# Gated delta-rule attention in one megakernel: outputs and gates with channels on the partitions, square sums in column tiles, roots spread by DMA

## The chip, the core and the metric

The kernel runs on one core of a Trainium2 chip, as one program. Its metric is the device time of one execution, in microseconds (us). The core has five engines that run side by side: TensorE (PE in the profile, with PEld for its weight loads), VectorE (DVE), ScalarE (ACT), GpSimd (POOL), and SyncE (SP), which here only issues DMA transfers. Each engine takes its instructions in the order in which they were written. Everything is float32.

## The reference, cut to what matters

The input x has 4 sequences of 256 tokens with 256 channels; the attention sees it as 2 sequences of 512. The first layer's attention is a chunked gated delta rule with 16 key heads and 32 value heads of 128 channels. Its end is what the change concerns:

```python
core = chunk_gated_delta_rule(q, k, v, g, beta)
out = core * rsqrt(mean(core * core, -1, keepdims=True) + EPS) * norm_w
out = out * silu(z)                 # z = x @ w_z, one gate per output channel
return out.reshape(Bb, Ss, VAL_DIM) @ w_out
```

Around it stand "conditioning" steps (a two-way scan over time that gives a ratio by which a sigmoid of x is multiplied), a mixture of 64 small experts, a gated mixing layer and a mixture of 8 experts. The results are added to x.

## The kernel before

**Tiling.** The 1024 tokens are two halves s = 0, 1 of 512 tokens (two sequences b of 256, each two chunks n of 128). A `Unit` is one key head with its two value heads v in one half: 32 units. Four units are a `Group`, and two consecutive units are a pair that shares the inverse of the triangular matrix and the output projection. Tiles are 128 partitions by 512 elements.

**One unit.** `products` loads `wqk`, makes q and k with channels on the partitions (`convolved`: matmul `ps_cvq`, `ps_cvk`, then a scaled copy on ACT and three taps on DVE), applies silu, makes the products of q and k (`ps_gram`), and takes the square sums of q and k by matmuls of 32 columns of ones (`ps_kt`, four column tiles), turned by a DVE transpose of 32x32 blocks. It also builds the decay matrices `attnT` from a broadcast read of `G`. `values` makes v in the same way, transposes it on PE (`ps_vt`) so that tokens stand on the partitions, and scales it by `kn` into `vo`. `outputs` runs the delta rule: `ps_vn`, copied to `vn`; `ps_at` for chunk 0, copied over `vo[0]`; `vd` (POOL); `ps_ks`; `ps_vn` for chunk 1; `ps_at` for chunk 1 (two products per problem), copied over `vo[1]`. Tokens are on the partitions in all of these. The gates `zs` come from `gates`: matmul `ps_z` with tokens on the partitions, then silu on ACT. For a few units of the first half (`EARLY`) they are made early, stored and read back.

`normed` takes square sums on ACT (eight activations with accumulation into `rs`, through `junko`), adds `eo` and takes the power -1/2 on POOL, multiplies `vo` by the roots and then by `zs` on POOL, and transposes on PE (`ps_ot`); ACT copies the result to `oT`, scaled by `normw`, with channels on the partitions. `Group.project` multiplies `oT` by `wo` for both units of a pair (`ps_wo`, eight matmuls of 512 columns) and DVE adds the result to x.

**The order.** Nothing is issued as it is written in the code. Every step is an `op` of a `Tape` with its engine, its cost, the buffers that it reads and writes, sometimes a due time and an activation table. `Tape.plan` places all steps by their urgency, with weights in a line of constants (`SWITCH`, `SPARE`, `IDLE`, `THIN` and others), 59 shared buffers of 128x512 (`PLACES`, with a limit for each use in `MOST`) and six PSUM buffers; `pushed` works out new urgencies from the plan, and `run` repeats this `ROUNDS` times and takes one of the plans. Then all steps are issued in the order of their planned starts, and the engines keep that order. The planned times are only used for the order. Since every step is recorded through one helper, all rows of the profile show its line, and steps are told apart by their tiles.

The rest of the program (`Rest`: experts, mixing) is planned on the same tape; that of the first half fills the time beside the attention of the second half, and that of the second half ends the program.

Of the kernel before, what the change touches and what calls it, by code (L numbers as in the profile page):

```python
# [12 lines left out]
ALU = mybir.AluOpType  # L13
# [168 lines left out]
class Tape:  # L182
# [222 lines left out]
    def run(self):  # L405
        latest, plans = self.urgency(), []
        for n in range(ROUNDS):
            last = self.plan(latest)
            if last is None:
                break  # L410
            plans.append((last, n, [(o.start, o.end, o.new) for o in self.ops]))
            latest = self.pushed(last)
        for o, (o.start, o.end, o.new) in zip(self.ops, min(plans)[2]):
            pass
        for o in sorted(self.ops, key=lambda o: (o.start, o.order)):
            for buf in o.new:
                buf()
            o.emit()


ROUNDS, SWITCH, LOAD, SPARE, AHEAD, EACH, END, IDLE, MOMENT, GAP, RATE, GIVES = 10, 14.532, 1.3, 95.787, 163.973, 23.222, 1300.0, 54.829, 0.668, 62.664, 3.14, 4.877
UNIT = 42

EARLY, FEW = range(3, 5), 6
NORMS = 0.55
FOUR32, TWO64 = 0.75, 1.1
LAND = 3.0
WINDOW, ENOUGH, LITTLE, SLOW, THIN = 3.4, 0.471, 0.38, 0.5, 6.598


def _mm(n, count=1):
# [4 lines left out]
def _act(n):  # L436
    return 0.2 + 0.00078 * n


def _dve(n):  # L440
    return 0.16 + 0.00104 * n
# [354 lines left out]
class Unit:  # L796
# [85 lines left out]
    def products(self):  # L882
# [104 lines left out]
            v.reciprocal(ki().rearrange("p n b -> p (n b)"), k2())  # L987
            v.tensor_scalar(self.eo(), sums(1), 1e-6, 1e-6 * P * P, ALU.add, ALU.mult)

        op("DVE", 0.78, shifted, [ps], [turned, k2, ki, self.eo])  # L990
        op(
            "POOL",
            1.03,
# [95 lines left out]
    def values(self):  # L1089
# [17 lines left out]
        for n in range(2):  # L1107
            vo = self.buf([P, 2, 2, P], "vo", 4, name=n)
            self.vo.append(vo)
            ps = p.ps(f"vt{n}_{self.tag}")  # L1110

            def turn(n=n, ps=ps):
                for v in range(2):
                    for b in range(2):
                        at = (2 * v + b) * P
                        e.tensor.transpose(
                            ps()[:, at : at + P], accs[v]()[:, b, n * P : n * P + P], p.const(IDENT)
                        )

            op("PE", 0.44, turn, accs, [ps], to=vo)  # L1120

            def scaled(n=n, ps=ps, vo=vo):
                norms = self.kn()[:, 2 * n : 2 * n + 2].unsqueeze(1).unsqueeze(3)
                e.vector.tensor_tensor(
                    vo(),
                    ps().rearrange("p (v b d) -> p v b d", v=2, b=2),
                    norms.to_broadcast([P, 2, 2, P]),
                    ALU.mult,
                )

            op("DVE", _dve(512), scaled, [ps, self.kn], [vo])

    def outputs(self):
        p, s = self.p, self.s
# [37 lines left out]
        def decayed():  # L1172
# [1 line left out]

        op("POOL", 1.06, decayed, [vn0, self.dc], [vd])
        ps = product(
            "at0",
            lambda q: self.attnT[0]()[:, q, :],
            lambda q: vn0()[:, q, :],
            [self.attnT[0], vn0],  # L1180
        )
        copied(lambda: vob(0), ps, vo[0])
        ps = product(
            "ks",
            lambda q: cross()[:, 0, q % 2, :],
            lambda q: vd()[:, q, :],
# [36 lines left out]
        op("POOL", 1.28, queries, [cross], [qe])  # L1223
        self.zs = self.gates()
        vn1 = new_values(1, lambda: vob(1), vo[1])
        ps = p.ps(f"at1_{self.tag}")

        def second():
            for q in range(4):
                o = ps()[:, q * P : q * P + P]  # L1230
                e.tensor.matmul(o, qe()[:, q, :], vd()[:, q, :], start=True, stop=False)
                e.tensor.matmul(o, self.attnT[1]()[:, q, :], vn1()[:, q, :], start=False, stop=True)

        op("PE", 2 * cost, second, [qe, vd, self.attnT[1], vn1], [ps])
        copied(lambda: vob(1), ps, vo[1])

    def gates(self, early=False):

# [1 line left out]
        e, op = p.e, p.tape.op  # L1240
        of = []
        if self.kept:
            for n, (kept, keptb) in enumerate(self.kept):
                zs = self.buf([P, 2, 2, P], "zs", 3, name=n)
                op(
                    "SP",
                    0.45,
# [5 lines left out]
                of.append(zs)  # L1253
            return of
        wz = self.load("wz", early=early)
        for n in range(2):
            zs = self.buf([P, 2, 2, P], "zse" if early else "zs", 3, name=n)
            of.append(zs)
            ps = p.ps(f"z{n}_{self.tag}")

            def products(n=n, ps=ps):
                for b in range(2):
                    for k in range(2):
                        e.tensor.matmul(
                            ps()[:, b * 256 : b * 256 + 256],
                            p.tokens(4 * s + 2 * b + n)[:, k, :],
                            wz()[:, k, :],
                            start=k == 0,
                            stop=k == 1,
                        )  # L1270

            op("PE", _mm(256, 4), products, [wz, p.actb[s]], [ps], to=zs, few=early)

            def silu(zs=zs, ps=ps):
                e.scalar.activation(
                    zs().rearrange("p v b d -> p b v d"),
                    ps().rearrange("p (b v d) -> p b v d", b=2, v=2),
                    AF.Silu,
                )

            op("ACT", _act(512), silu, [ps], [zs], table="silu")
        return of

    def early(self):

        p = self.p
        for n, zs in enumerate(self.gates(True)):
            name = f"zs{n}_{self.tag}"
            kept = p.dram.tile([P, 2, 2, P], F32, name=name, tag=name)
            keptb = p.stays(name)  # L1290
            p.tape.op(
                "SP",
# [8 lines left out]
    def normed(self):  # L1301


        p = self.p
        e, op = p.e, p.tape.op
        vo, zs = self.vo, self.zs
        tt = e.gpsimd.tensor_tensor
        junk = self.buf([P, P], "junko", 1)
        rs = self.buf([P, 2, 2, 2], "rs", 3)

        def o(n):
            return vo[n]().rearrange("p v b d -> p (v b) d")

        def roots(n):
            return rs()[:, n].rearrange("p v b -> p (v b)")

        for n in range(2):

            def squares(n=n):
                for q in range(4):  # L1320
                    e.scalar.activation(
                        junk(), o(n)[:, q, :], AF.Square, accum_out=roots(n)[:, q : q + 1]
                    )

            op("ACT", 1.71, squares, [vo[n]], [junk, (rs, {n})])

        def shifted():
            eps = self.eo().rearrange("p (n b) -> p n b", n=2)
            tt(rs(), rs(), _over(eps, 2, 2), ALU.add)

        def root():
            flat = rs().rearrange("p n v b -> p (n v b)")
            tt(flat, flat, p.neghalf, ALU.pow)

        op("POOL", 0.22, shifted, [self.eo], [rs])
        op("POOL", 1.64, root, [], [rs])
        for n in range(2):
            op(
                "POOL",
                1.06,  # L1340
                lambda n=n: tt(o(n), o(n), _over(roots(n), 2, P), ALU.mult),
                [rs],
                [vo[n]],
            )
            op(
                "POOL",
                1.28,
                lambda n=n: tt(
                    o(n), o(n), zs[n]().rearrange("p v b d -> p (v b) d"), ALU.mult
                ),  # L1350
                [zs[n]],
                [vo[n]],
            )
        self.oT = []
        for v in range(2):
            oT = self.buf([P, 512], "oT", 4, name=v)
            self.oT.append(oT)
            ps = p.ps(f"ot{v}_{self.tag}")

            def turn(v=v, ps=ps):  # L1360
                for b in range(2):
                    for n in range(2):
                        at = (2 * b + n) * P
                        e.tensor.transpose(
                            ps()[:, at : at + P], vo[n]()[:, v, b, :], p.const(IDENT)
                        )

            op("PE", 0.44, turn, vo, [ps], to=oT)
            op(
                "ACT",  # L1370
                0.69,
                lambda oT=oT, ps=ps: e.scalar.activation(oT(), ps(), AF.Copy, scale=p.normw),
                [ps, p.normwb],
                [oT],
            )
        self.wo = self.load("wo", 2)


class Program:
# [79 lines left out]

    PLACES = 59  # L1460

    MOST = {'attnT': 20, 'kq1': 12, 'kq0': 2, 'kqm': 17, 'cross': 10, 'vo': 18, 'zs': 5, 'oT': 6, 'w0': 5, 'hw0': 9, 'w1': 8, 'hw1': 7, 'wo': 2, 'sq': 4, 'r0': 10, 'wqk': 20, 'vn': 21, 'acck': 22, 'wb0': 3, 'vd': 7, 'U': 5, 'wv': 7, 'qe': 6}

    def place(self, use, name, shape=(P, 512)):

# [55 lines left out]
    def ratio_piece(self, c, cc, b):  # L1521
# [51 lines left out]
        def both_ways(src, extra, n):  # L1573
            fw, bw = new(f"fw{n}"), new(f"bw{n}", f"bw{n}" if summed else "bw")
            op(
                "DVE",
                0.95,
                lambda: v.tensor_tensor_scan(fw(), decay, src(), 0.0, ALU.mult, ALU.add),
                [src, self.decayb],
                [fw],  # L1580
            )
            op(
                "DVE",
                0.95,
                lambda: v.tensor_tensor_scan(
                    bw()[:, ::-1], decay, src()[:, ::-1], 0.0, ALU.mult, ALU.add
                ),
# [669 lines left out]
```

## Time and profile before

| | us |
|---|---|
| median of 3 runs (lowest to highest) | 1409.51 (1408.84 to 1413.2) |
| the profiled execution's own time | 1412.93 |
| its span, first to last instruction | 1411.1 |
| TensorE's mean granted clock | 0.982 of full speed |

A row of the profile's groups gives an engine, an operation, the tile that is written and those that are read (buffer numbers left out), the shape, the count, the busy time with the mean of one in ns, and the idle time of that engine just before them. A row of DMA issues gives the count, the size of each, and the median time from issue to landing. The chain is followed back from the last instruction to what released it.

### The profile page before, as it was taken

What the parts mean: (1) busy time and instruction counts of PE and PEld (TensorE: products, weight loads), DVE (VectorE), ACT (ScalarE), POOL (GpSimd) and SP (SyncE); (2) the same over time, 40 slices, a digit from 0 to 9 for tenths busy, and PEclk for the clock granted to TensorE, in tenths of its full rate; (3) what the DMA queues carried; (4) which work ended last, traced back from release to release, by engine and by line L of the source; (5) the groups of instructions that cost most, each with busy time, mean ns of one, the idle gap of its engine ahead of it and who ended that gap; (6) DMA issues with size and microseconds to landing.
All of it is one profiled execution on the core that took longest, in us unless ns stands there. A gap on an engine that the chain in (4) does not pass through costs nothing.

```text
span 1411.1 us, 24205 instructions
## 1 busy us (share of the span) xinstructions
PE 1321.2 (94%) x8428; PEld 817.4 (58%) x8428; DVE 1064.8 (75%) x2112; ACT 915.2 (65%) x1999; POOL 922.8 (65%) x913
## 2 busy tenths in 40 slices
PE   5986999999999899999999999999999999998988
PEld 3544766765875676766676576555455544443433
DVE  7889798787699588768769879867796787773123
ACT  1797799999889899988898898533434622211220
POOL 3189769979763988976885884487654666762032
PEclk9997999999999999999999999999999999999989
DMA  6412524412322353241351343544532324656030
GB/s 208 129 46 64 128 83 113 125 62 67 91 90 58 71 140 106 50 139 39 94 139 38 76 124 101 150 127 135 153 105 83 103 92 139 181 139 212 0 105 15
DMA packets 149817, 145.39 MB, mean 103 GB/s; under 512 B 76976, under 2 KB 93104, under 8 KB 149696
## 3 DMA queue, kind: packets, MB, share of 16 engines
q1 hardware_dynamic: 149264, 143.45, 35.5%
q8 instruction: 67, 1.10, 0.3%
q14 instruction: 54, 0.44, 0.1%
q10 hardware_dynamic: 432, 0.40, 0.1%
HBM read 129.75 MB, written 14.06 MB: 102 GB/s over the span
## 4 chain that ended last, share of the span: by engine, by line
PE 45%; DVE 25%; ACT 12%; POOL 7%; DMA 6%; issue 5%; SPq 1%; ACTq 0%; POOLq 0%; DVEq 0%
PE ps_h L128 5%; PE ps_a L128 4%; PE ps_ae L128 4%; PE ps_wo L128 4%; PE ps_e L128 4%; PE ps_z L128 4%; DVE xs L128 3%; DVE prod L128 3%; DVE accv_v L128 3%; PE ps_cvv L128 3%; PE ps_at L128 2%; DVE accq_q L128 2%; POOL attnT L128 2%; DMA w_w<-in_w 2%; ACT L128 2%
## 5 line engine op out<-in xcount | busy, mean ns | idle before, releaser
L128 ACT ACT_TABLE_LOAD x126 | 161.7, 1283 | 22.2 <-DVE sb_xT L128 10.4
L128 DVE SCALAR_TENSOR_TENSOR accv_v<-ps_cvv,sb_convw,accv_v 128x510 f32<-128x510 f32 (+2 forms) x192 | 141.8, 744 | 42.3 <-ACT accv_v L128 37.4
L128 PE MATMUL ps_z<-wz,ratio 128*128 128x256 f32 x480 | 118.7, 394 | 9.6 <-DVE vo L128 6.6
L128 POOL TENSOR_TENSOR hw_h<-hw_h,r_h 128x512 f32<-128x512 f32 x64 | 85.7, 1347 | 63.9 <-DVE hw_h L128 63.3
L128 PE MATMUL ps_h<-ratio,w_w 128*128 128x512 f32 x256 | 118.9, 598 | 6.6 <-DMA w_w<-in_w 5.7
L128 PE MATMUL ps_cvv<-ratio,wv 128*128 128x512 f32 x256 | 119.9, 601 | 2.9 <-ACT kqm L128 1.0
L128 ACT ACTIVATE r_h<-ps_h 128x512 f32<-128x512 f32 x64 | 38.2, 596 | 126.8 <-PE ps_h L128 126.5
L128 PE MATMUL ps_a<-hw_h,w_w 128*128 128x512 f32 x256 | 118.2, 593 | 0.0
L128 PE MATMUL ps_wo<-oT,wo 128*128 128x512 f32 x256 | 113.0, 593 | 0.0
L128 POOL TENSOR_TENSOR hw_e<-hw_e,r_e 128x512 f32<-128x512 f32 x32 | 41.6, 1322 | 101.0 <-DVE hw_e L128 101.0
L128 PEld LDWEIGHTS ps_z<-wz,ratio 128*128 128x128 f32 x480 | 90.1, 196 | 24.6 <-DVE vo L128 6.8
L128 PEld LDWEIGHTS ps_h<-ratio,w_w 128*128 128x128 f32 x256 | 47.0, 190 | 70.2 <-issue 55.1
L128 DVE TENSOR_TENSOR xs<-xs,prod 128x30 f32<-128x30 f32 (+14 forms) x240 | 81.2, 338 | 8.2
L128 DVE TENSOR_TENSOR prod<-xs,Rt 128x30 f32<-128x30 f32 (+14 forms) x240 | 78.5, 327 | 11.6 <-ACT xs L128 5.9
L128 ACT ACTIVATE junko<-vo 128x128 f32<-128x128 f32 x256 | 79.3, 310 | 7.6
L128 PE MATMUL ps_at<-vn,attnT 128*128 128x128 f32 x512 | 82.3, 277 | 1.5 <-ACT vn L128 1.4
L128 POOL TENSOR_TENSOR X<-attnT,kqm 128x512 f32<-128x512 f32 x64 | 82.8, 1313 | 1.2 <-ACT kqm L128 1.0
L128 POOL TENSOR_TENSOR vo<-vo,zs 128x512 f32<-128x512 f32 x64 | 81.2, 1288 | 1.6 <-ACT zs L128 1.6
L128 PEld LDWEIGHTS ps_wo<-oT,wo 128*128 128x128 f32 x256 | 48.1, 190 | 57.4 <-issue 52.6
L128 POOL TENSOR_TENSOR attnT<-attnT,sb_consts 128x512 f32<-128x512 f32 x56 | 70.7, 1280 | 15.5 <-DMA attnT<-G 8.5
L128 POOL TENSOR_TENSOR attnT<-attnT,kqm 128x512 f32<-128x512 f32 x64 | 80.6, 1278 | 0.1
L128 PEld LDWEIGHTS ps_a<-hw_h,w_w 128*128 128x128 f32 x256 | 47.9, 190 | 56.2 <-issue 52.6
(253 smaller groups left out, 3412.5 us busy)
## 6 DMA issues: line engine op xcount, KB each, us to landing
attnT<-G SPq DMA_DIRECT2D x64, 256.0 KB, 5.2
w_w<-in_w SPq DMA_DIRECT2D x64, 256.0 KB, 4.4
wb_wb<-w_rows SPq DMA_DIRECT2D x128, 128.0 KB, 3.6
wqk<-in_wqk SPq DMA_DIRECT2D x32, 256.0 KB, 4.2
wv<-in_wv SPq DMA_DIRECT2D x32, 256.0 KB, 4.2
wo<-in_wo SPq DMA_DIRECT2D x32, 256.0 KB, 3.8
qe<-G SPq DMA_DIRECT2D x32, 256.0 KB, 4.5
wz<-in_wz SPq DMA_DIRECT2D x30, 256.0 KB, 4.6
```

Of the source, the lines that this page charges most:

```text
L128: return self._tc.keep_in_program_order(f(*a, **k))
```

## The change

The outputs of the attention are made with channels on the partitions from the start, and what follows is done in that layout:

- `outputs`: the products `ps_at` have the value as the stationary operand, so that the output's channels land on the partitions. There is one PSUM tile for each value head v, holding both sequences and both chunks. Both are made after the second chunk's `vn`, in six matmuls each, and stay in PSUM; the copies to `vo` are gone.
- `gates`: `ps_z` has the weights as the stationary operand, in two matmuls of 512 columns for each v (four of 256 for each chunk before). `EARLY` has three units where there were two.
- `normed`: ACT squares both PSUM tiles whole (`sqo`). PE sums the squares over channels with 32 columns of ones in four column tiles (`ps_on`), and DVE turns the sums with a 32x32 block transpose and adds `eo`. POOL takes the power. SP writes the 8 x 128 roots to DRAM in single words, and reads them back twice, each time 512 roots spread over all partitions (`rb`). DVE makes `oT` from PSUM, `normw` and `zs`, and POOL multiplies it by `rb`. The transposes `ps_ot` are gone.
- `values`: the scaling by `kn` moves from DVE to ACT, in two activations of 256 columns for each chunk.
- The planner: other constants, other limits in `MOST`, some other costs; two rounds in place of ten, and the last plan in place of the one with the earliest end.

```diff
-        for o, (o.start, o.end, o.new) in zip(self.ops, min(plans)[2]):
+        for o, (o.start, o.end, o.new) in zip(self.ops, plans[-1][2]):
...
-EARLY, FEW = range(3, 5), 6
+EARLY, FEW = range(3, 6), 3
...
+            def evicted(n=n, ps=ps, vo=vo):
+                for b in range(2):
+                    e.scalar.activation(
+                        vo()[:, :, b, :],
+                        ps().rearrange("p (v b d) -> p v b d", v=2, b=2)[:, :, b, :],
+                        AF.Copy,
+                        scale=self.kn()[:, 2 * n + b : 2 * n + b + 1],
+                    )
...
-            op("DVE", _dve(512), scaled, [ps, self.kn], [vo])
+            if n in (0, 1):
+                op("ACT", 0.75, evicted, [ps, self.kn], [vo])
+            else:
+                op("DVE", _dve(512), scaled, [ps, self.kn], [vo])
...
+        for v in range(2):
+            ps = p.ps(f"at{v}_{self.tag}")
+            self.out.append(ps)
+            def heads(v=v, ps=ps):
+                for b in range(2):
+                    q = 2 * v + b
+                    for n in range(2):
+                        o = ps()[:, (2 * b + n) * P : (2 * b + n) * P + P]
+                        last, vn = self.attnT[n]()[:, q, :], (vn0, vn1)[n]()[:, q, :]
+                        if n:
+                            e.tensor.matmul(
+                                o, vd()[:, q, :], qe()[:, q, :], start=True, stop=False
+                            )
+                        e.tensor.matmul(o, vn, last, start=not n, stop=True)
...
+            def products(v=v, ps=ps):
+                for k in range(2):
+                    e.tensor.matmul(
+                        ps(),
+                        wz()[:, k, v * P : v * P + P],
+                        p.act[s][:, k, :],
+                        start=k == 0,
+                        stop=k == 1,
+                    )
...
+                lambda ps=ps, sq=sq: e.scalar.activation(sq(), ps(), AF.Square),
...
+        def norms():
+            for v in range(2):
+                for g in range(4):
+                    at = _quarter(g)
+                    e.tensor.matmul(
+                        sums()[at, v * P : v * P + P],
+                        p.ones,
+                        sqs[v]().rearrange("p (x t) -> p x t", t=P)[:, :, at],
+                        start=True,
+                        stop=True,
+                    )
...
         def shifted():
-            eps = self.eo().rearrange("p (n b) -> p n b", n=2)
-            tt(rs(), rs(), _over(eps, 2, 2), ALU.add)
+            v_.transpose(turned().rearrange("p x t -> p (x t)"), sums()[:, :256])
+            v_.tensor_tensor(
+                rs().rearrange("p (v b n) -> p v b n", v=2, b=2),
+                turned()[:, :, 0].rearrange("p (v b n) -> p v b n", v=2, b=2),
+                _over(self.eo().rearrange("p (n b) -> p b n", n=2), 1, 2),
+                ALU.add,
+            )
...
+        op("POOL", 1.64, lambda: tt(rs(), rs(), p.neghalf, ALU.pow), [], [rs])
...
+            lambda: e.sync.dma_start(out=rows.rearrange("x t -> t x"), in_=rs()),
...
+                lambda ps=ps, zs=zs, oT=oT: v_.scalar_tensor_tensor(
+                    oT(), ps(), p.normw, zs(), ALU.mult, ALU.mult
+                ),
...
+            def spread(v=v, rb=rb):
+                row = rows.rearrange("(v x) t -> v (x t)", v=2)[v : v + 1]
+                e.sync.dma_start(out=rb(), in_=row.to_broadcast([P, 512]))
+            op("SP", 0.45, spread, [rowsb], [rb], late=3.5)
+            op("POOL", 1.28, lambda rb=rb, oT=oT: tt(oT(), oT(), rb(), ALU.mult), [rb], [oT])
```

## The prediction, made before the changed kernel ran

> **What bounds the kernel now.** I read the page first: the engines' busy time and the chain that ended last.
>
> ```profile
> span 1411.1 us, 24205 instructions
> PE 1321.2 (94%) x8428; PEld 817.4 (58%) x8428; DVE 1064.8 (75%) x2112; ACT 915.2 (65%) x1999; POOL 922.8 (65%) x913
> PE 45%; DVE 25%; ACT 12%; POOL 7%; DMA 6%; issue 5%; SPq 1%; ACTq 0%; POOLq 0%; DVEq 0%
> ```
>
> PE is busy for 1321 of 1411 us, so at most 90 us of idle time can be won without giving PE less to do. The chain is PE for only 45%, with DVE second. To see whether that makes DVE the bound, I asked for busy time in stretches of 50 us (columns: stretch, its length, then PE, PEld, DVE, ACT and POOL busy, granted clock, DMA share, GB/s).
>
> ```profile
> 400.00:450.00 50.00, 49.22 (x257) 32.97 (x256) 47.37 (x102) 42.60 (x95) 24.61 (x25) 1.00 0.19 61
> 500.00:550.00 50.00, 49.51 (x381) 36.51 (x379) 44.80 (x107) 46.95 (x124) 42.08 (x40) 1.00 0.40 111
> 800.00:850.00 50.00, 47.16 (x529) 36.42 (x529) 40.85 (x77) 45.25 (x95) 42.41 (x46) 1.00 0.36 101
> ```
>
> In the attention, PE has 47 to 49.5 us of work in 50, with DVE and ACT right behind at 41 to 47. All are kept full by the written order, and PE is fullest: over the fifteen stretches from 150 to 900 us it is busy 720 of 750. So I price the change by PE's work first, and by what it does to the 30 idle us second.
>
> PE's busy figure includes pipelining, so I take the spacing from the first matmul of a group to the first of the next, in the timeline of PE. A float32 matmul has two records, a transpose one.
>
> ```profile
> 519.87 1.04 PE L128 MATMUL ps_ot<-sb_consts,vo 128*128 128x128 f32 x8
> 520.74 1.88 PE L128 MATMUL ps_cvq<-ratio,wqk 128*128 128x512 f32 x4
> 522.46 7.03 PE L128 MATMUL ps_wo<-oT,wo 128*128 128x512 f32 x16
> ...
> 567.02 0.65 PE L128 MATMUL ps_kt<-sq,ones 128*32 128x128 f32 x16
> 567.60 3.70 PE L128 MATMUL ps_cvv<-ratio,wv 128*128 128x512 f32 x8
> ...
> 593.45 1.99 PE L128 MATMUL ps_z<-wz,ratio 128*128 128x256 f32 x8
> 595.28 1.95 PE L128 MATMUL ps_vn<-vo,X 128*128 128x128 f32 x16
> ```
>
> Eight output transposes hold PE 0.87 us here, four records of a 512-wide product 1.72, sixteen of column-tiled sums 0.58, eight of a 256-wide gate product 1.83. Over the whole trace I worked out the medians of such spacings: 0.95, 1.72, 0.57 and 1.83 us.
>
> **PE's work, per head.** The eight transposes go: -0.95. The column-tiled square sums come, the same shape and count as the ps_kt group: +0.57. The two gate products go from 256 to 512 wide: 2 x (1.72 - 1.83) = -0.22. The attention products keep twelve matmuls of 128 columns (4 + 8 before, 6 + 6 after): 0. Sum -0.60 us, and 32 heads make -19.2. Bounds: with the shortest spacings for what goes (0.87; gates 1.73) and the mean, waits included, for the sums (0.77), -0.12 a head, -4 us; with the means for what goes (1.23; gates 1.98 against 1.83) and 0.57 for the sums, -0.96 a head, -31. I take the medians, because PE's queue is seldom empty here.
>
> **The other engines.** Their rows (busy, mean ns, idle before):
>
> ```profile
> L128 ACT ACTIVATE junko<-vo 128x128 f32<-128x128 f32 x256 | 79.3, 310 | 7.6
> L128 ACT ACTIVATION_READ_ACCUMULATOR junko<-vo 128x1 f32 x256 | 47.8, 187 | 0.0
> L128 POOL TENSOR_TENSOR vo<-vo,rs 128x512 f32<-128x512 f32 x64 | 66.8, 1065 | 2.4
> L128 DVE TENSOR_TENSOR vo<-ps_vt,kn 128x512 f32<-128x512 f32 x64 | 42.1, 682 | 4.6 <-PE ps_vt L128 4.0
> ```
>
> ACT loses the square sums (79.3 + 47.8), the 64 copies out of ps_at (36.8) and 64 of oT (40.4): 204.3 us. It gains 64 squares of 0.62 (row sq<-kq), 39.7; 128 scaled evictions of 256 columns, bounded by kq's 0.41 and by 0.50 (kq's plus the 0.085 by which accv_v<-ps_cvv, with a per-partition scale, exceeds r_h<-ps_h), and I take 0.50, 63.4; and 26 more table loads (152 in the built program against 126) at the measured 1.283, 33.4. Net -68 us. POOL loses 66.8 and the 7.6 of the small sum; its 64 multiplications by zs become 64 by rb at the same 1.28: -74. DVE loses 42.1 and gains 64 oT products of 0.751 (wb_z<-ps_mix, same shape), 48.1, 32 transposes of 0.443, 14.2, and 32 small sums between 0.18 (ki) and 0.40 (k), taken at 0.30, 9.6: +30. In most stretches that lies beside PE; where DVE stands at 47 of 50 it doesn't, and the cover is gone. If as much of it shows as DVE has of the chain, a quarter, it costs 7 us, at worst 30; at best nothing. Against it stand ACT's 68 us, of which PE waited for some. I let the two cancel and keep both in the range.
>
> **The new road.** Before, a head's last product waited for a copy, the square sums, three POOL steps and the transposes. Now, after the sums: DVE 0.44 + 0.30, POOL's power 1.65, SP's write of 1024 single words, SP's two broadcast reads of 256 KB, two POOL products of 1.29. The word write isn't in the trace; the nearest are
>
> ```profile
> attnT<-G SPq DMA_DIRECT2D x64, 256.0 KB, 5.2
> qe<-G SPq DMA_DIRECT2D x32, 256.0 KB, 4.5
> raw<-X SPq DMA_DIRECT2D x32, 128.0 KB, 3.2
> G<-rows SPq DMA_DIRECT2D x2, 64.0 KB, 1.5
> ```
>
> 1.5 us from below, 3.2 from above (also 1024 pieces, so nearer; Rt<-raw, 5.4, is the far end and belongs to the rival below); issue 0.33 to 0.62 each. The reads are shaped like attnT and qe, 4.5 to 5.2. So the road takes between 11.6 and 14.6 us without queueing. In the built order PE has, between the sums of a pair's second head and that pair's projection, 10.4 to 15.9 us of its own work (median 13.6, priced with the spacings above), and the projection needs the last oT only in its fourth matmul, 2.6 us later. That leaves four of the sixteen pairs short, by 1.6 + 1.1 + 0.8 + 0.7 = 4.2 us at the longer road, by nothing at the shorter. I take +2. The first head of each pair has 17.6 us or more.
>
> The Trainium skill's "DMA: Bandwidth & Descriptors" (Specifications) asks for at least 512 B per transfer, since smaller ones become a read-modify-write; it speaks against the word write. The trace's 128-byte pieces already break the rule and land in 3.2 us. The page gives no time for it, so by the rule I would only lean to the longer road, +4.2 in place of +2.
>
> SP issues 96 more transfers here, 3 x 0.38 x 32 = 36 us on a queue that has room (657 issues). But it is in order: the write waits there for POOL, the reads for the write's landing, and behind them stand the next loads of wv, wo, wqk, attnT and the inverses' blocks. Before, SP already waited 162 us behind ratio pieces and 116 behind X with little harm to PE; so I price this at nothing, and at up to the rival below if loads come late. The reads' 16.8 MB raise 145 MB by 12%, hidden at a 35% share. The third early head adds two stores and two loads, hidden likewise. The first attention product moves behind the second vn, which lets ps_ks start 0.9 us sooner and hides in the same order. The two ps_at banks are held until DVE's oT, but two ps_ot banks go and one comes: nothing. The retuned order keeps its outline: about 257 us of PE work still follow the last ps_wo.
>
> **Sum.** -19.2 + 2 = -17.2 on the profiled execution's 1412.9 (its span and 1.8 around) is 1395.7; it lay 3.4 above the median of the runs, so 1392.3. I forecast 1392, 1378 to 1406 by the bounds.
>
> **Rivals.** *The road is longer than its cover (slower).* All sixteen projections wait. It wins where the road exceeds the median cover, 13.6 + 2.6 = 16.2 us, by more than 17/16 = 1.1 us, so from 17.3 us. With attnT's longest landing, 8.5, the road is 17.9; with one POOL operation of 1.3 queued ahead, 19.2, which is 3.0 x 16 = 48 us: 1440. For it: POOL and SP serve in order, and POOL is over 90% busy in the stretch from 250 to 300 us. Against: DMA engines are 35% busy.
>
> *ACT was what held PE.* ACT stands at 42 to 47 of 50 us through the attention, and 68 us less lets PE recover half of its 30 idle us: 1392 - 15 = 1377. Against: waits of PE for ACT are small, the longest group 7 us.
>
> *A wash.* DVE's 30 us show in the inverse stretches by half, 15 us: 1407. For: DVE has 25% of the chain. Against: PE is still fuller there.
>
> That the change doesn't do what it says is excluded by the built program: all 32 heads have the sums, the write and both reads, and no transposes of outputs.
>
> **Chances.** A difference under 0.3% (4.2 us) can't be told from none. Forecast 0.50, long road 0.22, ACT 0.15, wash 0.13. Faster: 0.48 + 0.15 + 0.05 of the wash and 0.02 of the road = 0.70. Same: 0.02 + 0.05 + 0.03 = 0.10. Slower: 0.17 of the road and 0.03 of the wash = 0.20. The range 1370 to 1420 takes the forecast, most of the ACT case, the wash and the mild end of the road, 0.8 together; for the forecast alone it is 1378 to 1406.
>
> **What would show it.** Right: PE busy falls by 15 to 25 us with the idle time as before, 512-wide gates at 1.72, ps_on at 0.57, the write landing in under 3.2 us, and PE's waits for POOL's oT below 5 us in all. The road theory: PE idle before ps_wo, released by POOL oT, 2 us or more for each pair, and POOL idle before oT on the reads of rs. The ACT theory: PE idle from 150 to 900 us falls below 20. The wash: PE idle on DVE grows in the stretches with the inverses. I am wrong outright if PE's busy time doesn't fall, or if loads behind the reads reach PE late.

## The result: 1603 us, 14% slower

The changed kernel takes 1603.15 us, median of four runs (1600.32 to 1613.8). The kernel before, on the same chip, took 1409.17 (1407.52 to 1413.2). The ratio is 1.139, 95% interval 1.136 to 1.141. The forecast was 1392 with a range up to 1420. The loss of 194 us lies far outside, and the rival that ended on the slower side, priced at 1440, saw only a part of it.

The profiled execution took 1605.76 us. Its page: engines, granted clock, and the shares of the chain that ended last.

```profile
span 1604.0 us, 23928 instructions
PE 1378.5 (86%) x8428; PEld 775.7 (48%) x8428; DVE 1102.2 (69%) x2176; ACT 865.0 (54%) x1577; POOL 838.4 (52%) x817
PEclk8998989999998989999998899997999989999989
PE 42%; DMA 21%; DVE 16%; POOL 7%; ACT 6%; issue 5%; SPq 2%; another core or an unknown queue 0%; ACTq 0%; POOLq 0%; DVEq 0%
DMA rs<-rs 8%; DMA rb<-rs 6%; PE ps_wo L128 5%; PE ps_h L128 4%; DMA w_w<-in_w 4%; PE ps_ae L128 3%; PE ps_a L128 3%; PE ps_e L128 3%; PE ps_at L128 3%; PE ps_gram L128 3%; SPq L128 2%; PE ps_z L128 2%; PE ps_vn L128 2%; PE ps_cvv L128 2%; PE ps_in L128 2%
```

Of the chain, 21% are DMA, where it was 6%; the roots' word write (rs<-rs) alone has 8% and their reads (rb<-rs) 6%. PE has less work and is busy for 57 us more. That is no contradiction: its clock falls again and again (the digits of 7 and 8 in the middle of PEclk, where the work used to be steady), and at a lower clock the same matmuls are busy for longer.

The three stretches of 50 us shown of before, now (PE, PEld, DVE, ACT and POOL busy, granted clock, DMA share, GB/s):

```profile
400.00:450.00 50.00, 45.08 (x380) 27.62 (x379) 31.08 (x64) 33.16 (x57) 35.19 (x35) 0.97 0.30 68
500.00:550.00 50.00, 41.48 (x373) 24.53 (x374) 35.33 (x53) 32.22 (x75) 34.16 (x35) 0.86 0.43 117
800.00:850.00 50.00, 44.33 (x465) 29.32 (x462) 31.53 (x59) 35.66 (x65) 34.61 (x35) 0.97 0.40 93
```

PE has fallen from 47 to 49.5 busy microseconds to 41 to 45, and DVE and ACT from 41 to 47 to 31 to 36. No engine has become the bound; all of them wait. The groups of waits say for what (us in total, times, longest):

```profile
POOL oT L128 <- DMA rb<-rs: 202.0, 37, 13.6
PEld ps_wo L128 <- POOL oT L128: 95.0, 29, 11.1
PE ps_wo L128 <- POOL oT L128: 69.7, 15, 10.2
ACT xs L128 <- DMA Rt<-raw: 54.7, 6, 10.6
PE ps_h L128 <- DMA w_w<-in_w: 19.2, 12, 10.4
```

The first three are the new road: POOL waits for the roots' reads, and PE for POOL. The last two have nothing to do with the attention's outputs, and they have grown as well, from 3.7 and 5.7 us before. That is the first sign that more than a road is at fault: transfers of other parts come late too. (Not all of this growth is the words': with the short write of runs32, below, these two waits are still 18.1 and 12.9 us.)

One pair in the timeline of SP, POOL and PE (start, length, what, idle before it and its releaser):

```profile
472.07 0.38 SPq L128 DMA_DIRECT2D rs<-rs  x1
480.74 2.95 SPq L128 DMA_DIRECT2D rb<-rs  x2
488.54 0.37 SPq L128 DMA_DIRECT2D rs<-rs  x1
497.19 0.80 SPq L128 DMA_DIRECT2D rb<-rs  x2
```

```profile
485.63 1.29 POOL L128 TENSOR_TENSOR oT<-oT,rb 128x512 f32<-128x512 f32 x1 [13.59 <-DMA rb<-rs]
...
502.04 2.48 POOL L128 TENSOR_TENSOR oT<-oT,rb 128x512 f32<-128x512 f32 x2 [10.07 <-DMA rb<-rs]
```

```profile
496.00 3.52 PE L128 MATMUL ps_wo<-oT,wo 128*128 128x512 f32 x4 [1.45 <-issue]
...
503.36 8.39 PE L128 MATMUL ps_wo<-oT,wo 128*128 128x512 f32 x12 [3.85 <-POOL oT L128]
```

From the issue of the word write to that of the reads, which wait for its landing, pass 8.67 and 8.65 us. Over all 32 heads it is 8.5 to 14.5, median 10.6. The road from a head's sums to its second product takes 20.0 to 32.8 us, median 24.9, where 11.6 to 14.6 had been forecast. PE starts the projection, stops after its first records, and does the last twelve in 8.39 us, which is 0.70 each where before sixteen took 7.03: it has come out of the wait at half clock. Up to 509.4 us, when the clock is back, these records start 0.85 us apart, and then 0.43. By the trace's clock records PE spends 226 us at half clock, 53 before. These records change between 1.0 and 0.5 in steps of 3.41 us, which agrees with the Trainium skill's "TensorE: Matmul & The Clock Gate" (What's actually happening): half rate after an idle window of about 3.4 us. The waits of up to 10.2 us above are long enough for that.

### The profile page after: what moved, and what is told of

The parts are those of the page before. It is cut to its first block, busy times and chain, and to the rows that moved or that the text cites. A ratio compares the mean times of both kernels' runs of the same rounds, so it can differ in the third digit from the quotient of the medians.

```text
span 1604.0 us, 23928 instructions
## 1 busy us (share of the span) xinstructions
PE 1378.5 (86%) x8428; PEld 775.7 (48%) x8428; DVE 1102.2 (69%) x2176; ACT 865.0 (54%) x1577; POOL 838.4 (52%) x817
## 4 chain that ended last, share of the span: by engine, by line
PE 42%; DMA 21%; DVE 16%; POOL 7%; ACT 6%; issue 5%; SPq 2%; another core or an unknown queue 0%; ACTq 0%; POOLq 0%; DVEq 0%
DMA rs<-rs 8%; DMA rb<-rs 6%; PE ps_wo L128 5%; PE ps_h L128 4%; DMA w_w<-in_w 4%; PE ps_ae L128 3%; PE ps_a L128 3%; PE ps_e L128 3%; PE ps_at L128 3%; PE ps_gram L128 3%; SPq L128 2%; PE ps_z L128 2%; PE ps_vn L128 2%; PE ps_cvv L128 2%; PE ps_in L128 2%
## 5 line engine op out<-in xcount | busy, mean ns | idle before, releaser
L128 ACT ACT_TABLE_LOAD x152 | 195.0, 1283 | 28.1 <-DVE sb_xT L128 6.2
L128 PE MATMUL ps_wo<-oT,wo 128*128 128x512 f32 x256 | 143.4, 709 | 74.6 <-POOL oT L128 69.7
L128 POOL TENSOR_TENSOR oT<-oT,rb 128x512 f32<-128x512 f32 x64 | 81.2, 1281 | 202.3 <-DMA rb<-rs 202.0
L128 DVE SCALAR_TENSOR_TENSOR accv_v<-ps_cvv,sb_convw,accv_v 128x510 f32<-128x510 f32 (+2 forms) x192 | 141.7, 743 | 29.7 <-ACT accv_v L128 24.9
L128 PE MATMUL ps_h<-ratio,w_w 128*128 128x512 f32 x256 | 122.4, 611 | 20.9 <-DMA w_w<-in_w 19.2
L128 PEld LDWEIGHTS ps_wo<-oT,wo 128*128 128x128 f32 x256 | 55.4, 226 | 157.9 <-POOL oT L128 95.0
L128 PE MATMUL ps_z<-ratio,wz 128*128 128x512 f32 x232 | 115.2, 631 | 6.2 <-ACT vo L128 5.6
L128 DVE SCALAR_TENSOR_TENSOR hw_h<-ps_h,wb_wb 128x512 f32<-128x512 f32 x64 | 43.6, 683 | 72.7 <-ACT r_h L128 59.3
L128 POOL TENSOR_TENSOR rs<-rs,neghalf 128x8 f32<-128x8 f32 x32 | 53.5, 1673 | 69.7 <-DVE rs L128 59.0
L128 PE MATMUL ps_at<-attnT,vn 128*128 128x128 f32 x512 | 84.6, 278 | 2.1 <-ACT vn L128 2.1
L128 DVE SCALAR_TENSOR_TENSOR accq_q<-ps_cvq,sb_convw,accq_q 128x510 f32<-128x510 f32 (+2 forms) x96 | 71.3, 743 | 15.2 <-ACT accq_q L128 12.7
L128 ACT ACTIVATE attnT<-attnT,nG 128x128 f32<-128x128 f32 x224 | 70.5, 391 | 20.2 <-POOL attnT L128 20.0
L128 DVE TENSOR_TENSOR sb_xT<-sb_xT,ps_wo 128x512 f32<-128x512 f32 x32 | 21.9, 683 | 86.3 <-PE ps_wo L128 86.3
```

Source lines behind the costliest of these rows:

```text
L128: return self._tc.keep_in_program_order(f(*a, **k))
```

## The experiments

Sixteen kernels. For the table I measured, in each trace, how much of PE's time goes beyond its work: the start of a group of matmuls to the start of the next, less the shortest tenth of such spacings for that kind. "Half clock" is the time in which half the clock was granted.

| run | time, us | against before (95%) | half clock, us | PE beyond its work, us |
|---|---|---|---|---|
| before | 1409 to 1412 | | 53 | 134 |
| changed | 1603 | 1.139 (1.136 to 1.141) | 226 | 329 |
| runs32 | 1446 | 1.026 (1.024 to 1.029) | 93 | 174 |
| turned4 | 1452 | 1.030 (1.027 to 1.032) | 97 | 181 |
| nodep | 1572 | 1.116 (1.113 to 1.119) | 192 | 299 |
| late10 | 1590 | 1.129 (1.124 to 1.135) | 219 | 317 |
| words64 | 1455 | one run | 86 | 182 |
| before_neww | 1459 | 1.034 (1.030 to 1.037) | 93 | 189 |
| before_main | 1475 | 1.044 (1.040 to 1.049) | 102 | 198 |
| turn_b | 1413 | 1.002 (0.999 to 1.004) | 77 | 142 |
| turn_e | 1408 | 0.999 (0.997 to 1.001) | 73 | 140 |
| word_b | 1545 | 1.096 (1.092 to 1.100) | 193 | 279 |

The last column accounts for the time, though not to the microsecond: from before to the changed kernel it grows by 195 us and the time by 194, but from before to before_neww, where PE's work is the same, it grows by 55 and the time by 48.

### The write: length, wait, or the words themselves

**runs32.** The order and all else stay; only the write has pieces of 32 bytes in place of single words.

```diff
-            lambda: e.sync.dma_start(out=rows.rearrange("x t -> t x"), in_=rs()),
+            lambda: e.sync.dma_start(
+                out=rows.rearrange("x t -> (x t)").rearrange("(t x) -> t x", x=8), in_=rs()
+            ),
```

> The changed kernel in its very order, but the roots are written as they lie, 128 pieces of 32 bytes in place of 1024 words; they then stand in another order in DRAM, so the values that are read back belong to other tokens. Theory W (the landing of the scattered words, a median of 10.6 us from the write's issue to the reads' issue in the changed kernel's trace, where the prediction took 1.5 to 3.2, is the cause): the reads are issued 2 to 3 us after the write, the road from the square sums to the last product with the roots falls from 24.9 us to about 17, and the time to 1390 to 1425. Theory O (the new order of all steps is the worse one): the time stays above 1550. Theory Q (any wait of the in-order transfer queue for a landing starves the loads behind it): 1450 to 1530, with loads late.

Measured: 1445.85, so 157 us of the 194 hang on the shape of this one transfer. SP and POOL in its timeline:

```profile
426.61 0.33 SPq L128 DMA_DIRECT2D rs<-rs  x1
428.01 0.80 SPq L128 DMA_DIRECT2D rb<-rs  x2
```

```profile
431.28 1.27 POOL L128 TENSOR_TENSOR oT<-oT,rb 128x512 f32<-128x512 f32 x1 [4.70 <-DMA rb<-rs]
```

The reads go out 1.4 us after the write (median 1.5). The road's median is 15.5 us, and a projection has its 6.96 us again. PE's weight loads wait 2.1 us in all for POOL's oT, where it was 95.0. The remaining 36 us are another matter; see the order, below.

**nodep.** The words are still written, but the reads take rows of G, so nothing waits for the write.

```diff
-                row = rows.rearrange("(v x) t -> v (x t)", v=2)[v : v + 1]
-                e.sync.dma_start(out=rb(), in_=row.to_broadcast([P, 512]))
+                row = p.G[self.s][v : v + 1, 4 * self.h : 4 * self.h + 4, :]
+                to = rb().rearrange("p (x t) -> p x t", t=P)
+                e.sync.dma_start(out=to, in_=row.to_broadcast([P, 4, P]))
```

> The changed kernel in its very order, with the word write still made; but the two reads take rows of G, written long before, so they don't wait for the write (the outputs are multiplied by other values than the roots). Theory W: the road is short and the queue isn't held, 1375 to 1400. If the word writes also disturb other transfers while they are under way, theory D, it stays 20 us or more above the kernel with 32-byte pieces. Theory O: above 1550.

Measured: 1571.88. Without the wait only 31 us come back. Its timeline of SP and POOL shows why:

```profile
405.13 0.38 SPq L128 DMA_DIRECT2D rs<-rs  x1
405.60 1.01 SPq L128 DMA_DIRECT2D rb<-G  x2
```

```profile
418.80 1.44 POOL L128 TENSOR_TENSOR oT<-oT,rb 128x512 f32<-128x512 f32 x1 [4.73 <-DMA rb<-G]
```

The reads leave 0.5 us after the write, and their product starts 13.2 us later (median 12.8 from the issue of a head's first read, against 5.4 in runs32). What the core's transfers moved in the meantime (the columns of the stretches above):

```profile
409.00:416.00 7.00, 7.00 (x51) 4.07 (x51) 5.26 (x12) 4.59 (x11) 1.68 (x1) 1.00 0.08 8
416.00:419.00 3.00, 3.00 (x8) 1.33 (x7) 2.93 (x9) 2.97 (x6) 0.20 (x1) 1.00 0.80 135
```

Both reads, of 256 KB each, are issued by 406.6 us. They trickle at 8 GB/s until 416 us, 11 us after the write's issue, and then run at 135. Averaged over the 32 heads, traffic falls from 88 to 100 GB/s between 2 and 6 us after the write's issue to 28 to 44 between 7 and 11, and is 110 to 146 in the five us that follow; in runs32 it is 101 to 133 between 7 and 11. So the write isn't only long: until it has landed, transfers issued behind it hardly move. The road is still 23.0 us long (median), although nothing waits for the words. Part of the late Rt and w_w comes from there too: their waits are 46.9 and 18.2 us here, 18.1 and 12.9 in runs32.

**late10.** The planner is told of 7.6 us more until the landing, so that more of PE's work stands between.

```diff
+        p.tape.extra[len(p.tape.ops) - 1] = 7.6
...
-                other.ready = max(other.ready, end + self.hop(o, other))
+                other.ready = max(other.ready, end + self.hop(o, other) + self.extra.get(o.order, 0.0))
```

> The changed kernel with its word write, but the planner places the reads 7.6 us later, by the landing that the trace shows; PE's own work between a pair's sums and its projection rises from a median of 13.6 us to 18.8 (priced with the trace's spacings). Theory W with the late projection as its main effect: PE's wait before the projections falls by about 5 us for each of 16 pairs, 80 us or more off 1603, so 1490 to 1530. If instead the held queue is the main effect, it stays above 1560, since the wait for the landing is as long as before.

Measured: 1590.44. The cover grew from 13.6 to 18.8 us, and PE's projections ran through again (2.9 us of waits for POOL's oT, where it was 69.7), but the road grew too, to 30.9, and PE lost the time elsewhere (317 us beyond its work, against 329). So the longer cover didn't help. Why isn't shown: the held transfers are one reason, but all steps also stand in another order, and an order can cost tens of us by itself (below).

**words64.** Is it the number of pieces, or that neighbours lie close? Again 1,024 words, each 64 bytes from the next. A read of one word waits for the landing, then come the reads of G.

```diff
-        rows, rowsb = p.dram.tile([8, P], F32, name=name, tag=name), p.stays(name)
+        rows, rowsb = p.dram.tile([8, P, 16], F32, name=name, tag=name), p.stays(name)
...
-            lambda: e.sync.dma_start(out=rows.rearrange("x t -> t x"), in_=rs()),
+            lambda: e.sync.dma_start(out=rows[:, :, 0].rearrange("x t -> t x"), in_=rs()),
...
+                if v == 0:
+                    e.sync.dma_start(out=p.dum, in_=rows[7:8, P - 1, 0:1])
```

> The changed kernel with each of the 1024 words in a 64-byte line of its own in DRAM; a read of one word waits for the landing, and the reads of the spread rows take G (outputs multiplied by other values). If the slow landing (10.6 us) comes from sixteen words that share a line, it falls below 4 us and the time to about 1450. If it comes from the number or the size of the pieces, the landing stays at 8 to 11 us and the time at 1570 to 1610.

Measured: 1454.82 in its one run.

```profile
431.62 0.38 SPq L128 DMA_DIRECT2D rs<-rs  x1
434.42 0.25 SPq L128 DMA_DIRECT2D dum<-rs  x1
434.72 0.80 SPq L128 DMA_DIRECT2D rb<-G  x2
```

The words have landed 2.8 us after their issue; over all heads it is 2.5 to 7.4, median 3.2. So 1,024 pieces of 4 bytes are cheap, their median at the far end of the forecast's 1.5 to 3.2 us, if they lie 64 bytes apart. Packed side by side, sixteen in 64 bytes and coming from sixteen partitions, they take 8.5 us and more and hold up the rest. Two pieces of 32 bytes in the same 64 (runs32) do no harm. Other distances were not tried. The spread words also cover 64 KB in place of 4; whether the shared 64 bytes count, the sixteen partitions that meet there or the small stretch as a whole is open, and what happens inside the memory no trace shows.

**nowrite** leaves the write out altogether (its line becomes `lambda: None`) and reads G.

> The changed kernel in its very order without the write of the roots: the transfer queue neither waits for POOL's power nor for a landing, and the two reads take rows of G (the outputs are multiplied by other values than the roots; 16.8 MB are still read). With 32-byte pieces the kernel took 1446 us and with the words but without the wait 1572. Theory D (the words keep the DMA engines busy and hold up all other transfers): the whole 126 us between 1572 and 1446 go, since no word is written. What is left above 1392 tells what the remaining 54 us of the 32-byte kernel are: if they are the road and the held queue, 1390 to 1410; if they are the order of the steps, DVE's and ACT's new work or the reads' traffic, 1435 to 1450.

Measured: 1456.64. Without any write it isn't faster than with the 32-byte one, so with a harmless write SP's wait for the roots costs nothing more. Of the road it says nothing: the median is 15.7 us here and 15.5 in runs32.

**turned4** makes the layout whole with a short write: VectorE turns the roots back by a 32x32 transpose, and four transfers write eight rows of 128 bytes each.

```diff
+        def write():
+            v_.transpose(p.backo, full)
+            for g in range(4):
+                e.sync.dma_start(
+                    out=rows[:, 32 * g : 32 * g + 32], in_=p.backo[32 * g : 32 * g + 8]
+                )
```

> The whole computation, in the changed kernel's order: after the power, DVE turns the roots back (one 32x32 block per 32 partitions) and they are written as 32 rows of 128 bytes, in four transfers of eight rows, in place of 1024 words. Theory W: the write lands in 2.5 to 4 us, the road is about 18 us and the time 1390 to 1430, against 1409 before: the change's own saving on PE shows, less what the road still costs. Theory Q: 1450 or more, because the queue now issues four transfers and still waits for their landing. Theory O: above 1550.

Measured: 1452.26. Ratio 1.030: the words are cured, and it is still some 40 us slower than before.

### The last 40 us: layout or order

**dve_runs32** is runs32 with the scaling of the values back on VectorE (`if n in ():` in place of `if n in (0, 1):`), which also makes a new order.

> The 32-byte pieces, and the scaling of the values goes back from ACT to DVE as before the change; the planner makes a new order for that (the roots stand in another order, so the values read back belong to other tokens). If ACT's two scaled evictions for each chunk (about 1.0 us where the planner counts 0.75) are what keeps PE waiting, the time falls from 1446 to 1415 to 1435. If they are not, it stays within 10 us of 1446, or rises because DVE has 42 us more.

Measured: 1466.07, ratio 1.039 (1.036 to 1.042). So there is no sign that ScalarE's new evictions cost anything; as the order is another one too, this run alone doesn't exclude it. turn_e, below, keeps them and is as fast as before.

**before_neww** is the kernel of before with the changed kernel's weights and limits in the planner (the constant lines, `MOST`, the choice of the plan), and no other change.

> The kernel before with the changed kernel's planner constants, limits and choice of plan, and nothing else: its steps are the old ones in another order. Theory O (these constants give an order with more waits by themselves): 1425 to 1445, and the change's constants explain 15 to 35 of the 37 us by which the 32-byte kernel is slower than before. If the constants don't matter: 1400 to 1418.

Measured: 1458.95. The old layout loses 48 us by the new weights alone. With the same weights, the new layout and a short write (runs32, 1446) is 13 us faster than the old layout (10 by the ratios to before, 1.026 and 1.034). That is one pair of orders: dve_runs32, also with these weights, is 7 us slower than before_neww.

**before_main** and **before_most** take these weights apart: one has only the new line from `ROUNDS` to `GIVES` (with the choice of the last plan), the other only the new `MOST`.

> The kernel of before, with only the planner's one line of main weights (ROUNDS to GIVES) and the choice of the last plan taken from the changed kernel; EARLY, FEW, NORMS, FOUR32, WINDOW and MOST stay. With all of the changed kernel's weights this layout took 1459. Theory 'main weights': most of those 48 us hang on this line, so 1440 to 1460. Theory 'allowances': MOST carries them, and this run stays within 10 us of 1411. If both matter, 1425 to 1440.

> The kernel of before, with only the allowances of buffers ahead (MOST) taken from the changed kernel. Theory 'allowances': 1440 to 1460, as with all weights. Theory 'main weights': within 10 us of 1411. It also shows how far any change of the order, without a change of work, moves the time.

Measured: 1474.91, ratio 1.044, and 1441.70, ratio 1.022 (1.018 to 1.025). Either one alone costs the old layout 31 to 64 us, and all the new constants together (48) less than the one line alone. So neither carries the loss by itself: the old weights fit the old layout as a set, and each of these steps away from it costs some tens of microseconds.

**turn_a** and **turn_b** give the new layout orders of its own: turned4 with the turn-back as a step of the plan, the planner's costs set to the durations of the traces, and two unlike sets of weights and limits. Of the costs, turn_a and turn_b share these lines:

```diff
-        op("DVE", 1.0, shifted, [ps], [turned, k2, ki, self.eo])
+        op("DVE", 1.37, shifted, [ps], [turned, k2, ki, self.eo])
...
-                op("ACT", 0.75, evicted, [ps, self.kn], [vo])
+                op("ACT", 1.0, evicted, [ps, self.kn], [vo])
...
-            op("SP", 0.45, spread, [rowsb], [rb], late=3.5)
+            op("SP", 0.45, spread, [rowsb], [rb], late=4.5)
```

> The changed kernel's layout with the roots turned back on VectorE by a 32x32 transpose and written as four transfers of eight rows of 128 bytes, and with an order of its own: the planner's costs set to what the traces show (value scaling on ScalarE 1.0 us, the keys' shifted sums 1.37, the scans 0.9, a read of the roots 1.3 + 4.5), its weights and allowances chosen for this kernel. Theory 'the order, not the layout, holds the last 40 us': with a fitting order this layout gains its 12 us of PE work over before, 1390 to 1410. Theory 'the layout itself costs' (long road, ACT's scaling, table loads): 1430 to 1455, as with the changed kernel's order (1452). In between, 1410 to 1430, both.

> The same layout and costs as the run before it in this list, with a second, unlike set of weights and allowances (nearer to the kernel of before: early heads 3 and 4 only). Theory 'order': 1390 to 1410 here too, and the two differ by under 15 us. Theory 'layout': 1430 to 1455. If the two differ by over 20 us, the order by itself moves the time by more than the layout's whole gain.

Measured: 1426.66, ratio 1.014 (1.008 to 1.020), and 1413.01, ratio 1.002 (0.999 to 1.004). turn_b is 39 us faster than turned4, and as fast as before. It has two early heads where turned4 has three; turn_a, which keeps three, is 26 us faster than turned4. So the layout doesn't have to cost the last 40 us: most of them were the order.

**word_b** is turn_b with the word write put back.

```diff
-            for g in range(4):
-                e.sync.dma_start(
-                    out=rows[:, 32 * g : 32 * g + 32], in_=p.backo[32 * g : 32 * g + 8]
-                )
+            e.sync.dma_start(out=rows.rearrange("x t -> t x"), in_=rs())
```

> The run turn_b (1413) with one thing put back: the roots go out as the changed kernel's 1,024 words instead of four times eight rows of 128 bytes. Order, weights and everything else stay (VectorE still turns the roots, and nobody reads that). Theory 'words in shared lines': they alone cost about what they cost between the changed kernel and its 32-byte twin, 1603 - 1446 = 157, so 1540 to 1580. Theory 'the order was what failed': a fitting order takes the long write with it, under 1450.

Measured: 1544.93. In a fitting order the words cost 132 us, little less than the 157 in the other. Its waits look like those of the changed kernel:

```profile
POOL oT L128 <- DMA rb<-rs: 164.2, 35, 12.3
PEld ps_wo L128 <- POOL oT L128: 61.4, 19, 11.9
PE ps_wo L128 <- POOL oT L128: 46.7, 7, 11.1
```

**turn_d**, **turn_e** and **before_d** ask how much is left to the order's chance: turn_b's weights moved a little in two ways, and before's moved a little.

> turn_b with weights and allowances moved a little further by the planner's own reckoning. Theory 'the layout has its 12 us of PE work to give, once the order fits': 1395 to 1408. Theory 'nothing left': the order moves it by a few us either way around 1413, 1408 to 1425.

> As turn_d, from another path of the same search. The same expectations: 1395 to 1408 if the layout's PE work can be had, 1408 to 1425 if not. Together with turn_d it shows how far near orders differ: if they lie more than 12 us apart, the layout's gain is smaller than what the order decides.

> The kernel of before with weights and allowances moved a little in the same way, its layout untouched. If orders near a fitting one all run alike, 1405 to 1415. If it runs at 1420 or above, the order of before is one of the best of its kind, and every other layout that has to leave it starts with a debt of that size.

Measured: turn_d 1416.28, ratio 1.004 (1.001 to 1.006); turn_e 1408.07, ratio 0.999 (0.997 to 1.001); before_d 1421.66, ratio 1.008 (1.006 to 1.011). Near orders differ by 8 to 12 us, about as much as the layout has to give. before_d, above 1420, is one sign that the order of before is among the best of its kind. turn_e is the fastest version with the new layout, and can't be told from the kernel of before. Its page:

```profile
span 1407.8 us, 24064 instructions
PE 1321.7 (94%) x8428; PEld 756.4 (54%) x8428; DVE 1110.6 (79%) x2209; ACT 865.1 (61%) x1576; POOL 849.9 (60%) x817
PEclk9989799999999999999999999999999999999999
```

PE is full again, and its busy time is that of before, 1321 us. By an estimate, most of the 13 us of saved work have gone to the clock: turn_e spends 73 us at half clock against 53, and 20 us at half speed cost some 10. PEclk shows the main place: an 8 in the third slice of 35 us and a 7 in the fifth. Of the 73 us 44 lie ahead of 180 us, of the 53 before 31.

## Why the prediction was wrong

**The step that failed: the price of the word write.** The prediction bounded it by 1.5 and 3.2 us, "also 1024 pieces, so nearer". That compared the number of pieces, and took pieces of 128 bytes for pieces of 4. words64 shows that the number was indeed not the point; what no row of before showed was words written side by side. The far end of 5.4 us was too low as well: 8.5 to 14.5. And it was priced only by its own landing, as one link of the road. nodep shows that the wait for it is the smaller part: 31 of 157 us come back when nobody waits for the words, because the reads issued behind them come late all the same.

**The rule that spoke against it.** The Trainium skill's "DMA: Bandwidth & Descriptors" (Specifications) asks for 512 bytes, for want of which a transfer becomes a read-modify-write. I let the 128-byte pieces, which break it and land in 3.2 us, speak for the words too, and leaned by 2 us. The warning was worth heeding, but 512 bytes is not where the loss begins here: pieces of 128 and of 32 bytes, and words 64 bytes apart, break the rule alike and cost next to nothing.

**The second failed step: "the retuned order keeps its outline", priced at nothing.** before_neww measured the new weights at 48 us on the old layout, more than twice the gain that was forecast. The order was taken as a frame for the sum, and was itself the second largest term.

**PE's work.** The sums by column tiles take 0.575 us by the same spacings (forecast 0.57), the transposes are gone. The gates were mis-sized: their 512-wide products reach 1.72 at the shortest, but the median is 1.81 (1.77 in turn_e) against 1.83 before, so two of them save 0.04 us a head and not 0.22. That leaves -0.95 + 0.575 - 0.04 = -0.41 a head, 13 us over 32 and not 19.2. At like weights runs32 and before_neww lie 13 us apart. That agrees, but may be luck, as orders differ by that much by themselves. PE's busy time, which was to fall by 15 to 25 us, rose by 57 with the clock, for which the sum has no term.

**The other engines.** ACT fell by 50 us (forecast 68), POOL by 84 (74), DVE rose by 37 (30); the 26 more table loads came (152, 195.0 us in all, 1.283 each). None of them is busy for more than 36 of 50 us in the stretches shown, and moving the scaling back, in an order of its own, gained nothing. The wash and the ACT rival are not what happened: from 150 to 900 us PE is idle for 109 us, where the ACT rival asked for under 20.

**SP's queue, priced at nothing.** Of SP's own waits in the changed kernel the longest group is

```profile
SPq L128 <- DMA rs<-rs: 261.5, 30, 11.5
```

the reads that stand in line for the words' landing. Where the write is short, such waiting is harmless (nowrite is no faster than runs32). The price was right, as long as what SP waits for is short.

**The long road, the rival on the slower side.** Its signs came true: PE idle before ps_wo on POOL's oT, POOL idle on the reads of rs, and a road of 24.9 us, past its 17.3. It named the largest single part: PE's idle time (span less busy) is 225.5 us in the changed kernel and 108.9 in runs32, and 69.7 of these 116.6 us are waits of ps_wo for POOL's oT. What it had wrong was again the write's landing: by its own rule the measured road costs (24.9 - 16.2) x 16 = 139 us, not 48. But more cover was no cure: late10 took these waits away and gained 13 us of 194, in another order. How the 157 us divide between late projections and other late transfers stays open. A slow transfer was thought of as a link in one chain, and was a load on the transfers behind it too.

The chain of runs, then: 1411 before, +48 for the weights (before_neww), -13 for the layout (runs32), +157 for the words. These steps end at the measured 1603 by how they are laid out; whether they add up is told by other runs. word_b adds the words alone and gives +132. turn_b is rid of the words and of the unfit order; by the sum it should take 1398, and takes 1413, 15 us more, where near orders differ by 8 to 12. So the layout's own 13 us are seen in PE's spacings and in one pair at like weights, but not won in any version that ran. Left open are why the words cost 25 us less in turn_b's order, and the cost of the third early head, which was not tried alone.

## What to carry to other kernels

Price a scattered write by rows with the same size of piece and the same distance between pieces, and if there is no such row, let its range reach to a multiple; then ask what the transfer does to all others, and not only who waits for it. A short transpose on a compute engine that makes contiguous rows is a cheap cure (32 of 0.20 us here). Where a kernel's order comes from weights tuned for one layout, compare layouts under the same weights, and under more than one set: here the moves away from the tuned set cost 31 to 64 us and near orders differed by 8 to 12, where the layout had 13 to give.

## What the runs showed of the hardware

- 1,024 words written side by side into 4 KB of DRAM land in 8.5 to 14.5 us (median 10.6), and reads issued right behind them have their product start 12.8 us after their issue (median). Between 7 and 11 us after the write's issue the core's transfers move 28 to 44 GB/s, and over 100 afterwards. The same words 64 bytes apart land in 3.2 us, and 128 pieces of 32 bytes in 1.5 (medians).
- In the DMA records the words themselves end 1.5 us after the issue, in the packed case as in the spread one, where nothing else is under way. The rest of the 8.5 us shows in the landing, and in nodep in the packets of the reads behind them.
- Waits of PE of some microseconds cost more than their length: at half clock the records of ps_wo start 0.85 us apart, at full clock 0.43. By an estimate, half of the 226 us at half clock, some 110 of the changed kernel's 329 us beyond its work, are lost by that.
